# Feed-forward in groups of three for the last 33 blocks of a two-layer graph network, and one block alone at the end

## The chip, the core and the metric

The kernel runs on one core of a Trainium2 chip. The metric is device time in microseconds (us), from the first to the last instruction of one execution, as the median of several runs. Features and weights are float32.

## What is computed

There are 10000 nodes with 512 features each and 160000 edges. The edges are sorted by destination and have one of four types. The reference, cut to what matters:

```
h   = relu(layernorm(x))
# layer 0
m   = mean over edges into n of (h[src] @ rel_W[type] + rel_b[type])
x1  = layernorm(h + h @ self_W + self_b + m)          # scaled by ln1_w, ln1_b
f   = gelu(x1 @ W1 + b1) @ W2 + b2                    # 512 -> 1024 -> 512
x   = x + layernorm(x1 + f)                           # scaled by ln2_w, ln2_b
# layer 1
h   = relu(layernorm(x))
h   = relu(h @ W_self1 + mean(h[src]) @ W_neigh1 + b1)
out = x + relu(h @ W_self2 + mean(h[src]) @ W_neigh2 + b2)
```

## The kernel before

The nodes are cut into 78 blocks of 128 rows, numbered 0 to 77, and one block of 16 rows, number 78, which is taken first. The program has four stages. The first one multiplies all nodes by the four relation matrices, and writes the table `hall_d`; it also makes the lists of edges. The second stage, which the change touches, goes over the 79 blocks: it sums the messages of a block, applies the first layer norm, the feed-forward part (gelu) and the second layer norm, and writes the input of layer 1 to `h1_d`. The third and the fourth stage are the two steps of layer 1; each one gathers rows of a table that the stage ahead of it has written in full. So the third stage can gather nothing before the last row of `h1_d` has been written.

**Gathers.** For a block, `begin` (L900) calls `gather` (L840), which issues indirect DMAs on POOL (L844): 5 lists of rows that are summed with a one-hot matrix ("others"), 11 lists with one row per node ("mine"), and every fourth and every sixteenth block one further list that serves 4 or 16 blocks (`tails`; `halves_of`, L830, splits it into a high and a low part on DVE and ACT). Every list fills a tile `rows` of 128 rows by 2 KB; in the second stage there are 28 such tiles in turn (`RINGS`). TensorE (PE) sums the others into PSUM (`sums`, L881, with the matmuls in L897), and DVE adds the 11 mine (`add`, L904, with L908).

**Slots.** The order is written out by hand (the scheduler is off in this part). The loop over the blocks from L1164 on makes one slot per block b. A slot holds, in this order: the one-hot matrices for block b+1; `second` (L1097) for what came out of the feed-forward part in the slot before; `add` for block b; the statistics of its layer norm; `products` (L1143), which is one part of a queue of feed-forward work; within it, ahead of its last call, `scaled` (L1109), that is the layer norms on ACT and DVE and the writes of `xn_d` and `h1_d`; and `begin` for block b+1. In the middle of the work of the next slot block b is turned (four transposes on PE, L1018).

**Groups.** The feed-forward part works on groups of blocks (`Group`, L1005). `up` (L1024) makes 128 of the 1024 hidden features for all blocks of the group: four matmuls with n = 128 columns per block (L1030), and one gelu on ACT (L1032). `down` (L1035) takes 8 matmuls with 512 columns per block (L1041). `parts` (L1045) cuts a group into parts, and each slot takes one part off the queue. Before, groups are four blocks; a group has four parts: 4 ups, 4 ups, 2 downs, 2 downs. A group's parts go into the queue at the end of the first slot of the next group. The last group holds blocks 76 and 77. `load_res` (L942) loads the residual rows ahead of a pair of downs; its three buffers are taken in turn.

After the loop the parts that are left are worked off (from L1201 on), with no more gathers beside them. Of the groups, the parts left at that point are: the three last parts of blocks 72 to 75 and the three parts of blocks 76 and 77.

Of the kernel before, what the change touches and what calls it, by code (L numbers as in the profile page):

```python
# [21 lines left out]
def kernel(  # L22
# [39 lines left out]
    FC = F // P  # L62
# [8 lines left out]
    full = N // P  # L71
# [528 lines left out]
    with ExitStack() as s:  # L600
# [42 lines left out]
        def turned(i, rows, c):  # L643

            r = sets[i][2]
            xg, sc, hg, hT = rows
            nc.scalar.activation(hg[:r, c, :], xg[:r, c, :], AF.Relu, bias=sc[c][1],
                                 scale=sc[c][0])
            transposed(psT, hT[:, c, :, :r], hg[:r, c, :], r)
# [162 lines left out]
    def aligned(ctxa):  # L812
# [5 lines left out]
        rest = list(range(full))  # L818
        blocks = ([full] if N % P else []) + rest

        def height(b):
            return min(P, N - b * P)
# [38 lines left out]
        def hots(b, pool, lanes=None):  # L861
            n = OT + NL if b < full else OT_LAST
            hot = pool.tile([P, OT + NL, P], F32, name="hot", bufs=2)
            if lanes is None:
                for t in range(n):
                    nc.scalar.activation(hot[:, t, :], lane, AF.Abs, bias=loc[:, b, t:t + 1],  # L866
                                         scale=-1.0)
                nc.scalar.activation(hot[:, :n], hot[:, :n], AF.Relu, bias=ones[:, :1], scale=-1.0)
                return hot
            nc.vector.tensor_tensor(hot[:, :n].bitcast(F32R),  # L870
                                    lanes[:, None, :].to_broadcast([P, n, P]),
                                    loc[:, b, :n].unsqueeze(2).to_broadcast([P, n, P]),
                                    op=OP.is_equal)
            return hot
# [25 lines left out]
        def begin(b, hot, table, pool, idle=None, split=False):  # L900
            others, mine = gather(b, table, pool, split)
            return sums(b, others, hot, idle), mine

        def add(b, pa, mine):  # L904

            r = height(b)
            for t in mine:
                nc.vector.tensor_tensor(pa[:r], pa[:r], t[:r], op=OP.add)  # L908


        with ExitStack() as s:
# [16 lines left out]
            def pair(t, b, n, name, bufs):  # L928

                return (gp.tile([P, 2, D], F32, name=name, bufs=bufs)[:height(b), :n],  # L930
                        rows_of(t, (b, n, height(b))))

            def load(b):
                if b < full and b % 2:
                    return
                n = 2 if b < full else 1
                v, at = pair(xs_d, b, n, "xs", 3)
                nc.sync.dma_start(v, at)
                for c in range(n):
                    nodes[b + c] = v[:, c, :]  # L940

            def load_res(b, n):  # L942
                i = len(taken) % 3
                taken.append(b)
                v, at = pair(xr_d, b, n, "xr", 1)
                if i:
                    v = halves[i - 1][:height(b), :n]
                nc.sync.dma_start(v, at)
                for c in range(n):
                    xrs[b + c] = v[:, c, :]  # L950
                xrs[b, n] = v
# [13 lines left out]
            def fetch(n, room=None):  # L965

                for k, b in enumerate(waiting[:n]):
                    i = late.index(b)
                    t = row_tile() if room is None else room[:, k, :]
                    queue = nc.sync if room is None else nc.scalar  # L970
                    queue.dma_start(t, hT_d[i * P:(i + 1) * P, :])
                    arrived.append((b, t))
                del waiting[:n]

            def residuals(n):

                for b, t in arrived[:n]:
                    po = psO.tile([P, D], F32, name="po")
                    for k in range(KC):
                        nc.tensor.matmul(po, t[:, k * P:(k + 1) * P], wself[:, k, :],  # L980
                                         start=(k == 0), stop=(k == KC - 1))
                    nc.vector.tensor_tensor(t, po, bself, op=OP.add)
                    nc.sync.dma_start(xs_d[b * P:(b + 1) * P, :], t)
                del arrived[:n]
# [20 lines left out]
            class Group:  # L1005
# [26 lines left out]
                    nc.scalar.activation(self.hid[:, f, :n], ph[:, :n], AF.Gelu,  # L1032
                                         bias=b1s[:, f:f + 1], scale=1.0)

                def down(self, b):  # L1035
                    c, r = self.bs.index(b), self.r
                    if c % 2 == 0:
                        load_res(b, min(2, len(self.bs) - c))
                    po = psO.tile([P, D], F32, name="po")
                    for f in range(FC):  # L1040
                        nc.tensor.matmul(po[:r], self.hid[:, f, c * r:(c + 1) * r], w2s[:, f, :],  # L1041
                                         start=(f == 0), stop=(f == FC - 1))
                    return b, po

                def parts(self):  # L1045

                    ups = [lambda f=f: self.up(f) for f in range(FC)]
                    downs = [lambda b=b: self.down(b) for b in self.bs]
                    return [ups[:FC // 2], ups[FC // 2:]] + [downs[i:i + 2]
                                                             for i in range(0, len(downs), 2)]  # L1050

            COLS = 8

            class Scales:
# [31 lines left out]
                def affine(self, out, v, c, r, w, to):  # L1086
# [3 lines left out]
                    nc.vector.scalar_tensor_tensor(out, v, self.rs[:r, 0, c:c + 1], to,  # L1090
                                                   op0=OP.mult, op1=OP.add)

            rests = {}
            fed, third = [], []
            now = Scales()
# [38 lines left out]
                    nc.sync.dma_start(rows_of(xn_d, (b, n, height(b))), xrs.pop((b, n)))  # L1134

            plan = [[b] for b in blocks[:len(blocks) - len(rest)]]
            plan += [rest[:-2][i:i + 4] for i in range(0, len(rest) - 2, 4)] + [rest[-2:]]
            queue = []
            turning = None
            held = begin(blocks[0], first_hot, table, gp, split=True)  # L1140
# [2 lines left out]
            def products(work, turned):  # L1143


                nonlocal fed
                got = []
                residuals(min(2, len(arrived) - len(ready)))
                for i, call in enumerate(work):
                    if i == len(work) - 1:  # L1150
                        yield
                    if i == len(work) // 2 and turned:
                        turned()
                    got.append(call())
                if not work:
                    yield
                    if turned:
                        turned()
                residuals(len(arrived) - len(ready))
                fed = [g for g in got if g]  # L1160

            i = 0
            grp = None
            for bs in plan:  # L1164
                for b in bs:
                    r = height(b)
                    if b == bs[0]:
                        before, grp = grp, Group(bs)
                    if i + 2 < len(blocks):
                        load(blocks[i + 2])  # L1170
                    if i + 1 < len(blocks):
                        hot = hots(blocks[i + 1], gp, lanes)
                    ready = []
                    if i + 2 < len(LATE):
                        if i:
                            fetch(LATE[i + 2])
                        ready = arrived[len(arrived) - LATE[i + 2]:]
                    if i == 1:
                        nc.sync.dma_start(w2s, w2.rearrange("(k p) n -> p k n", p=P))
                    got = second()  # L1180
                    pa, mine = held
                    add(b, pa, mine)
                    v = nodes[b]
                    nc.vector.scalar_tensor_tensor(pa[:r], pa[:r], rdeg[:r, b:b + 1], v[:r],
                                                   op0=OP.mult, op1=OP.add)
                    first = (b, now.stats(pa[:r], r), pa)
                    part = products(queue.pop(0) if queue else [], turning)
                    next(part)
                    now.finish()
                    scaled(got, first)  # L1190
                    next(part, None)
                    if i + 1 < len(blocks):
                        held = begin(blocks[i + 1], hot, table, gp, split=True)

                    if b == bs[0] and before:
                        queue += before.parts()
                    turning = lambda g=grp, b=b, v=v: g.turn(b, v)
                    i += 1
            turning()
            queue += grp.parts()  # L1200
            while queue or fed or third:  # L1201
                got = second()
                part = products(queue.pop(0) if queue else [], None)
# [9 lines left out]
        for step, (h_d, ws, wn, bs) in enumerate(((h1_d, ws1, wn1, bs1), (h2_d, ws2, wn2, bs2))):  # L1213
            with ExitStack() as s:
# [47 lines left out]
                before = None  # L1262
                held = begin(blocks[0], hots(blocks[0], ip), h_d, ip)
                for i, b in enumerate(blocks):
# [6 lines left out]
                    m = ip.tile([P, D], F32, name="mb")  # L1271
# [13 lines left out]
                    before = (b, po, mT)  # L1285
# [319 lines left out]
```

## Time and profile before

Every fp32 matmul of the program stands in the trace as two records.

| | |
|---|---|
| time, median of 3 runs | 6163.95 us (6160.82 to 6165.61) |
| profiled execution | 7032.07 us, span 7030.1 us, mean granted clock 0.904 |
| gathers (L844) | 3828 in all: 1716 + 858 + 786 + 393 + 50 + 25 |
| first gather of the second stage | 1206.0 us |
| last gather of the second stage ends | 3125.0 us |
| first gather of the third stage | 3239.43 us |
| pause of the gathers between the third and fourth stage | 60.07 us |
| last gather starts | 6970.74 us |

The profiled execution is longer than the runs without the profiler. The page gives busy time by engine over the whole span; the stretches of the second stage have to be read from the timeline, since the stages have different limits. "Idle before" is time that an engine spent waiting ahead of an instruction, with what ended it; "issue" is a wait for nothing that the profile shows.

### The profile page before, as it was taken

The page shows a single profiled execution, that of the slowest core. Times are in us where ns is not written, and L with a number is a line of the kernel's source. Part 1 is how long each engine was busy: PE and PEld are TensorE (multiplying, and loading weights), DVE is VectorE, ACT ScalarE, POOL GpSimd, SP SyncE. Part 2 cuts the span into 40 slices and gives each one's busy share as a digit, 9 for nine tenths or more (in the row PEclk, how much of TensorE's full clock was granted, in tenths as well). Part 3 has the DMA queues.
Part 4 walks back from the last instruction along what each step waited for, and adds up shares of the span by engine and source line. Part 5 has one row for each costly group of instructions (what it writes and reads, how often), then busy time and mean ns, then how long its engine had stood idle before and what let it go on. Part 6 is the DMA issues. An engine that isn't in the chain of part 4 may idle for free.

```text
span 7030.1 us, 55146 instructions
## 1 busy us (share of the span) xinstructions
PE 5756.5 (82%) x15103; PEld 2675.2 (38%) x15103; DVE 3683.9 (52%) x7447; ACT 1805.0 (26%) x3594; POOL 3716.9 (53%) x3927
## 2 busy tenths in 40 slices
PE   9999999788988889885777777777757777777778
PEld 4555544343433334332333333333323333333333
DVE  8889995466766667661333333333323343434334
ACT  1046660123222223221222222222212121212122
POOL 0011110566666666643666666666556666666664
PEclk9999999899999999997888888988878888898889
DMA  4333344777777777654666666666657676776764
GB/s 156 115 129 123 131 156 149 238 222 225 225 217 217 223 218 229 210 178 157 202 205 205 203 205 204 209 202 204 185 180 218 209 221 211 217 220 212 220 213 154
DMA packets 503502, 1373.79 MB, mean 195 GB/s; under 512 B 82206, under 2 KB 82206, under 8 KB 503054
## 3 DMA queue, kind: packets, MB, share of 16 engines
q0 software_dynamic: 308768, 1008.91, 47.8%
q1 hardware_dynamic: 192734, 358.11, 14.0%
q10 hardware_dynamic: 1680, 3.15, 0.1%
q8 instruction: 122, 2.00, 0.1%
q14 instruction: 198, 1.62, 0.1%
HBM read 1156.54 MB, written 213.30 MB: 195 GB/s over the span
## 4 chain that ended last, share of the span: by engine, by line
PE 61%; issue 19%; another core or an unknown queue 9%; DVE 5%; ACT 3%; DMA 2%; POOL 2%; SPq 0%; POOLq 0%; DVEq 0%; ACTq 0%
PE pa L897 14%; PE pm L774 13%; PE ph L1030 7%; PE po L1247 7%; PE po L1041 6%; PE po L1276 4%; PE pa L879 4%; DVE pa L908 3%; PE pm L678 2%; POOL rows L844 2%; PE pT L172 2%; PE po L980 1%; DMA rows<-h_d,row 1%; PE pT L1018 0%
## 5 line engine op out<-in xcount | busy, mean ns | idle before, releaser
L908 DVE TENSOR_TENSOR pa<-pa,rows 128x512 f32<-128x512 f32 x2574 | 1799.0, 699 | 2026.4 <-remote 1008.8
L844 POOL DMA_INDIRECT rows<-h_d,row x1716 | 1621.9, 945 | 1006.0 <-issue 381.8
L1247 PE MATMUL po<-wns,mTb 128*128 128x512 f32 (+1 forms) x1264 | 737.9, 738 | 836.5 <-issue 653.0
L897 PE MATMUL pa<-rows,hot 128*128 128x512 f32 (+1 forms) x2358 | 1116.1, 613 | 101.1 <-issue 91.1
L844 POOL DMA_INDIRECT rows<-hall_d,row x858 | 822.1, 958 | 497.0 <-issue 196.8
L844 POOL DMA_INDIRECT rows<-h_d,orow x786 | 743.0, 945 | 413.3 <-issue 222.1
L1247 PEld LDWEIGHTS po<-wns,mTb 128*128 128x128 f32 (+1 forms) x1264 | 290.2, 238 | 1270.5 <-issue 1043.6
L897 PEld LDWEIGHTS pa<-rows,hot 128*128 128x128 f32 (+1 forms) x2358 | 456.1, 194 | 706.6 <-issue 680.9
L1030 PE MATMUL ph<-x1T,w1s 128*128 128x512 f32 (+2 forms) x1344 | 582.5, 585 | 74.1 <-ACT hid L1032 37.1
L1276 PE MATMUL po<-wss,hTb 128*128 128x512 f32 (+1 forms) x1264 | 596.3, 616 | 39.6 <-issue 24.5
L1041 PE MATMUL po<-w2s,hid 128*128 128x512 f32 (+1 forms) x1264 | 581.3, 609 | 47.2 <-issue 45.1
L844 POOL DMA_INDIRECT rows<-hall_d,orow x393 | 373.2, 950 | 393.5 <-PE pm L678 203.4
L173 ACT COPY mTb<-pT 128x512 f32<-128x512 f32 (+1 forms) x158 | 91.8, 581 | 1769.5 <-remote 1381.7
L879 PE MATMUL pa<-wss,ident 128*128 128x512 f32 x936 | 427.5, 593 | 0.0
L1030 PEld LDWEIGHTS ph<-x1T,w1s 128*128 128x128 f32 x1344 | 255.5, 198 | 372.5 <-issue 319.3
L1041 PEld LDWEIGHTS po<-w2s,hid 128*128 128x128 f32 (+1 forms) x1264 | 239.5, 193 | 341.9 <-issue 337.3
L513 POOL DMA_INDIRECT win<-rec_d,at x79 | 81.5, 1031 | 529.0 <-PE pe L538 348.2
L1276 PEld LDWEIGHTS po<-wss,hTb 128*128 128x128 f32 (+1 forms) x1264 | 235.9, 197 | 293.1 <-issue 271.1
L866 ACT ACTIVATE hot<-lane,loc 128x128 f32<-128x128 f32 x1098 | 337.8, 392 | 0.0
L774 PE MATMUL pm<-wrel,hT 128*128 128x512 f32 x624 | 296.5, 597 | 0.0
L774 PE MATMUL pm<-wrel,s 128*128 128x512 f32 x624 | 293.3, 592 | 0.0
L897 PE MATMUL pa<-tail,hot 128*128 128x512 f32 x624 | 293.2, 592 | 0.0
(307 smaller groups left out, 6117.9 us busy)
## 6 DMA issues: line engine op xcount, KB each, us to landing
hall_d<-p SPq DMA_DIRECT2D x156, 256.0 KB
hall_d<-u SPq DMA_DIRECT2D x156, 256.0 KB
hb<-h_d SPq DMA_DIRECT2D x156, 256.0 KB
rows<-h_d,row POOLq DMA_INDIRECT x1716
xg<-in_x_dram SPq DMA_DIRECT2D x39, 512.0 KB
xr_d<-xg SPq DMA_DIRECT2D x39, 512.0 KB
xs<-xs_d SPq DMA_DIRECT2D x39, 512.0 KB
h_d<-h SPq DMA_DIRECT2D x39, 512.0 KB
```

The costliest lines, as they stand in the source:

```text
L172: nc.tensor.transpose(p[:, k, :r], rows[:, k * P:(k + 1) * P], ident[:r, :r])
L678: nc.tensor.matmul(pm, a[:, k, :], w[:, k, :], start=(k == 0), stop=(k == KH - 1))
L774: nc.tensor.matmul(pm, a[:, k, :], w[:, k, :], start=(k == 0), stop=(k == KH - 1))
L844: nc.gpsimd.indirect_dma_start(out=t[:n], out_offset=None, in_=table, in_offset=bass.IndirectOffsetOnAxis(ap=idx, axis=0))
L866: nc.scalar.activation(hot[:, t, :], lane, AF.Abs, bias=loc[:, b, t:t + 1], scale=-1.0)
L879: nc.tensor.matmul(p, ident, w, start=True, stop=True)
L897: nc.tensor.matmul(pa[:r], h, v, start=(i == 0), stop=(i == len(work) - 1))
L908: nc.vector.tensor_tensor(pa[:r], pa[:r], t[:r], op=OP.add)
L1030: nc.tensor.matmul(ph[:, :n], w1s[:, k, f * P:(f + 1) * P], self.xT[:, k, :n], start=(k == 0), stop=(k == KC - 1))
L1041: nc.tensor.matmul(po[:r], self.hid[:, f, c * r:(c + 1) * r], w2s[:, f, :], start=(f == 0), stop=(f == FC - 1))
L1247: nc.tensor.matmul(po[:r], mT[:, k, :r], wns[:, k, :], start=False, stop=(k == KC - 1))
L1276: nc.tensor.matmul(po[:r], hT[:, k, :r], wss[:, k, :], start=(k == 0), stop=False)
```

## The change

Blocks 0 to 43 stay in groups of four. Blocks 44 to 76 become eleven groups of three, and block 77 is a group alone. A group of three has three parts: 5 ups; 3 ups and one down; 2 downs. The residual rows are loaded for one block and then for two. A group of one has 4 ups, 4 ups, and one down. In addition a slot takes a second part where, after its first, the queue still holds at least as many parts as the group that was queued last has. That is so in one slot: in the slot of block 48 the last part of blocks 40 to 43 (2 downs) is followed by the first part of blocks 44 to 46 (5 ups).

```diff
-                def down(self, b):
+                def down(self, b, n=0):
                     c, r = self.bs.index(b), self.r
-                    if c % 2 == 0:
-                        load_res(b, min(2, len(self.bs) - c))
+                    if n:
+                        load_res(b, n)
...
                     ups = [lambda f=f: self.up(f) for f in range(FC)]
-                    downs = [lambda b=b: self.down(b) for b in self.bs]
-                    return [ups[:FC // 2], ups[FC // 2:]] + [downs[i:i + 2]
-                                                             for i in range(0, len(downs), 2)]
+                    odd, m = len(self.bs) % 2, len(self.bs)
+                    downs = [lambda b=b, n=(1 if i < odd else (i - odd + 1) % 2 * 2): self.down(b, n)
+                             for i, b in enumerate(self.bs)]
+                    if m == 3:
+                        return [ups[:5], ups[5:] + downs[:1], downs[1:]]
+                    return [ups[:FC // 2], ups[FC // 2:]] + [downs[i:i + 2] for i in range(0, m, 2)]
...
+            THREES = 11
+            assert (full - 1 - 3 * THREES) % 4 == 0
...
-            plan += [rest[:-2][i:i + 4] for i in range(0, len(rest) - 2, 4)] + [rest[-2:]]
+            cut = full - 1 - THREES * 3
+            plan += [rest[i:i + 4] for i in range(0, cut, 4)]
+            plan += [rest[i:i + 3] for i in range(cut, full - 1, 3)] + [rest[-1:]]
...
-            i = 0
+            i = newest = 0
...
-                    part = products(queue.pop(0) if queue else [], turning)
+                    work = queue.pop(0) if queue else []
+                    if len(queue) >= newest > 0:
+                        work += queue.pop(0)
+                    part = products(work, turning)
...
                     if b == bs[0] and before:
+                        newest = len(before.parts())
                         queue += before.parts()
```

## The prediction

> **What bounds the kernel now.** I read the page first, then the order of time on PE in one stretch of the second stage and at that stage's end, then POOL, then ACT at the end.
>
> ```profile
> span 7030.1 us, 55146 instructions
> PE 5756.5 (82%) x15103; PEld 2675.2 (38%) x15103; DVE 3683.9 (52%) x7447; ACT 1805.0 (26%) x3594; POOL 3716.9 (53%) x3927
> ```
>
> The shares are means over four stages, so they decide nothing here. The timeline of PE shows a slot (start, duration, idle before):
>
> ```profile
> 2653.38 7.03 PE L1030 MATMUL ph<-x1T,w1s 128*128 128x512 f32 x16
> 2660.25 0.60 PE L1018 MATMUL pT<-ident,xs 128*128 128x128 f32 x4
> 2660.68 7.03 PE L1030 MATMUL ph<-x1T,w1s 128*128 128x512 f32 x16
> 2667.15 0.80 PE L897 MATMUL pa<-upper,hot 128*128 128x512 f32 x1
> ...
> 2668.48 4.46 PE L897 MATMUL pa<-rows,hot 128*128 128x512 f32 x10
> 2672.77 7.03 PE L1030 MATMUL ph<-x1T,w1s 128*128 128x512 f32 x16
> ```
>
> From 2653.38 to 2672.77 PE never stops: a slot **needs 19.39 us of PE**. The stretch 2400 to 3139 us has 32.5 slots, 22.7 us each; 102 us of it are waits of PE of many kinds ("issue" most of all), the rest mostly records at half rate. So in the profiled execution PE is nearly the bound, with stops that no other engine's work explains.
>
> POOL is the other candidate:
>
> ```profile
> 3239.43 0.94 POOL L844 DMA_INDIRECT rows<-h_d,orow  x1 [114.43 <-DMA h_d<-h]
> 3240.68 0.94 POOL L844 DMA_INDIRECT rows<-h_d,orow  x1 [0.30 <-issue]
> ```
>
> One gather starts 1.25 us after the other. A slot has 16 gathers, and 1/4 and 1/16 for the shared lists: 16.31 x 1.25 = 20.4 us. This tells of the runs without the profiler too. Free of gathers are 1206.0 us at the start, 114.43, 60.07, and 59.4 at the end (7030.1 - 6970.74), in all 1440. With 3828 x 1.25 = 4785 that is 6225 us, which is already more than the median of 6164. So there the gathers can take **at most** (6164 - 1440) / 3828 = 1.234 us each on average, waits included, 20.13 us a slot, if the rest is as in the profile. Almost none of the profile's stops can then be left, and PE's 19.39 us stands just under POOL's 20.13. I take POOL as the pacer of a slot there, by 0.74 us at most.
>
> At the stage's end there is no gather, and PE works alone:
>
> ```profile
> 3139.09 7.03 PE L1030 MATMUL ph<-x1T,w1s 128*128 128x512 f32 x16
> ...
> 3154.11 13.90 PE L1030 MATMUL ph<-x1T,w1s 128*128 128x512 f32 x32
> 3167.84 27.63 PE L1041 MATMUL po<-w2s,hid 128*128 128x512 f32 x64
> 3195.31 3.62 PE L1030 MATMUL ph<-x1T,w1s 128*128 128x256 f32 x16
> 3199.10 5.45 PE L1030 MATMUL ph<-x1T,w1s 128*128 128x256 f32 x24 [0.18 <-ACT hid L1032]
> 3207.02 5.45 PE L1030 MATMUL ph<-x1T,w1s 128*128 128x256 f32 x24 [2.47 <-ACT hid L1032]
> 3212.31 13.90 PE L1041 MATMUL po<-w2s,hid 128*128 128x512 f32 x32
> ```
>
> The last sum (block 77) ends at 3139.09, the last down at 3226.2; ACT's last relu ends at 3235.7, and only then do h_d and, at 3239.43, the gathers follow. These **96.6 us are on the path** in full.
>
> **What the Trainium skill says.** "FP8 and Floating Point Precision", TensorE Precision Notes: true fp32 takes four passes through the array. The trace agrees so far as each matmul has two records; their spacing is what I use: 32 records in 13.90 us, the last lasting 0.59, are 0.429 us apart; 24 of n=256 in 5.45 (last 0.38) are 0.2205 apart. "TensorE: Matmul & The Clock Gate", What's actually happening: an idle window of about 3.4 us drops the array to half rate. The trace agrees: after the 2.47 us above the spacing stays 0.22, but after 3.64 us of waiting at 2716.89 weight loads come 0.85 apart. "ScalarE: Activation LUTs", What ACT_TABLE_LOAD costs: about 1283 ns; the trace has 1.28:
>
> ```profile
> 3201.63 1.28 ACT L1075 ACT_TABLE_LOAD   x1
> 3202.92 0.30 ACT L1075 ACTIVATE rs<-mv,eps 128x4 f32<-128x4 f32 x1
> 3203.66 1.52 ACT L1083 ACTIVATE h<-wself,rs 128x512 f32<-128x512 f32 x2 [0.45 <-DVE rs L1078]
> 3205.20 1.28 ACT L1032 ACT_TABLE_LOAD   x1
> ```
>
> Between two gelus stand two loads, the square root and the relus: that is what PE waits for at 3207.
>
> **The end, after.** Slot 77 now holds 2 downs (32 x 0.429 = 13.7) and two turns (0.9): 14.6. Blocks 74 to 76: 64 up records of n=384, which the trace lacks; between 0.2205 and 0.429 the line gives 0.325 (ends 0.32 and 0.34): 20.8. Their 48 down records: 20.6. Block 77 alone: 64 records of n=128: the line gives 0.117; the ups with n=16, 16 in 1.85 us, are 0.11 apart, which is the lower end, and the mean weight load of 0.19 the upper: 7.5 (7 to 12). Its down: 16 x 0.429 + 0.16 = 7.0. PE's sum is 70.5.
>
> Waits: now the ups of block 77 are shorter than ACT's work. From the start of its ups: first gelu (load 1.28, gelu about 0.37 between 0.27 for n=16 and 0.47 for n=256) at 2.9, third gelu at 4.5, load and root 6.1, DVE 0.4, one relu 0.78, load 1.28, fourth gelu ready at 9.0; the sixth up waits for it, some 3.3 us. So the last down ends at 18.8 instead of 14.5: 4.3 more, 6 if the gap brings half rate. Sum 74.8 against 87.1 before. Behind it, one block instead of two saves on DVE an affine pair and its statistics (0.75 + 0.75 + 0.87) and on ACT a relu (0.76), and may bare a table load (1.28): 9.5 becomes 7.1 to 8.4, 7.8. **The end shrinks from 96.6 to 82.6: by 14, 11 to 15 with the bounds; I take 13.**
>
> **What goes into the slots.** Ahead of the last sum the feed-forward work is that of 73 blocks instead of 72: 13.7 us. It enters in one place, the slot of block 48 (5 ups: 13.0). Triples cost 64 x 0.325 / 3 = 6.93 per block for ups, against 6.87: 30 x 0.06 = 1.9. **15.6 us more for PE**, with the slots of blocks 48 to 77, 30 of them, to win it back: 0.52 each. POOL's pace leaves 0.74 at most, 22 in all; 0.45 after 1% of other losses, 13.5, and 2 us remain late. I take 2.
>
> The added wait: the sum of block 49 stands 13 us later behind the second part; queued behind it on DVE is the add of block 49, and POOL waits for its tiles. The first tile is used again 28 gathers or 35 us later, and the sum could run about 12 us after it (7 gathers and a landing); 13 late leaves 10. The first mine tile is added about 31 us after the block's first gather and needed at 34 x 1.25 = 42. So POOL doesn't stop: zero; if that cover is thinner, up to 5.
>
> Transfers: ahead of 11 groups SP issues one load, one write of xn and one of h1 more, at 0.36 to 0.5 us, with the same bytes. The load for the single block now stands behind the writes of its slot on SP's queue, but is needed a slot later: zero beside SP's own waits for ACT's relu, the longest of which in 2400 to 3139 us lasts 36.8 us. ACT has 3 groups more of 8 gelus, but fewer table loads per block: zero under 26% busy.
>
> The sum on the profiled execution: 7032 - 13 + 2 = 7021; its stops blur the 2. The median is 868 us under it, but the end has no gathers and hardly any stops, so the same difference is set against the median: **6153**.
>
> **The rivals.**
> *PE paces the slots.* For it: the timeline, where PE runs back to back in most slots. Against: the bound of 1.234 holds for POOL only from above; if a gather takes under 1.19, PE's 19.39 is the larger. Then nothing is won back: 6164 - 13 + 15.6 = 6167; half won back 6159.
> *The split tails collide with the groups (slower).* Place: DVE. Blocks 52, 56, ... bring a new tail, whose halves come on DVE behind add (8.0), statistics (1.6), root with load (1.6), apply and affine (3): about 15 us after the last sum, while PE arrives after 14.2 + 4.3 = 18.5. With fours this slot has downs and no affines of fed blocks. With threes the slots of blocks 51, 63 and 75 have 5 ups, the root behind the fourth gelu (11.6), and two affine pairs with statistics (4.7): 21, against 17.8 for PE. 3 us each, 4.5 where two tails are split: 10 us, from the point where PE has no slack: 6167 + 10 = 6177. Where POOL paces, it is hidden.
>
> **How the numbers follow.** Forecast 6153, its own range 6147 to 6158: chance 0.54. PE paces: 0.34. Collision: 0.12. About 0.2% (12 us) is what a measurement of this kernel tells from no change; faster than 6151.6 is a little over half of the first case: 0.32. Slower than 6176.3 is two thirds of the collision: 0.08. The rest, 0.60, is within. The range 6147 to 6170 leaves out the collision and little else.
>
> **What would show it.** Right: the stretch from the last sum to the last relu is 82 to 86 us; the slot of block 48 has 27 us of products without a stop of POOL behind it; the sum of block 77 is no later than before by more than 2. Wrong: PE still behind at block 77 by over 10 us; DVE's halves awaited at blocks 52, 64 and 76; up records of n=384 over 0.34 apart; a gap in block 77's ups over 5 us.

## The result, and the profile after

The changed kernel takes **6148.31 us** (median of 12 runs, 6142.38 to 6151.56) against 6163.83 for the kernel before (12 runs, 6159.29 to 6167.8). The ratio is 0.9975, with a 95% interval of 0.9967 to 0.9983: 15.5 us less, between 10.5 and 20.3. The forecast was 6153, 11 us less, which lies inside that interval.

The first profile of the kernel before and experiments 5 to 12 fell where TensorE was granted less clock (0.90 on average instead of 0.98) and where the kernel before takes 7032 to 7053 us, so those runs are compared only with the kernel before run beside them; the profile of the kernel before that is used below (experiment 1) was taken at 0.979.

The page of the changed kernel:

```profile
span 6141.4 us, 55591 instructions
PE 5641.5 (92%) x15295; PEld 2602.8 (42%) x15295; DVE 3674.4 (60%) x7449; ACT 1800.9 (29%) x3615; POOL 3722.4 (61%) x3927
```

The count of PE's records has grown by 192 (blocks 44 to 77 are twelve groups instead of nine, with 64 up records each), its busy time has not. Where the time went is seen only in the two places that the change touches. The first is the slot of block 48, on PE (start, duration, what ran, idle before):

```profile
2235.30 14.00 PE L1041 MATMUL po<-w2s,hid 128*128 128x512 f32 x32 [0.38 <-DVE rest L1109]
2249.14 2.74 PE L1030 MATMUL ph<-x1T,w1s 128*128 128x384 f32 x8
2251.72 0.60 PE L1018 MATMUL pT<-ident,xs 128*128 128x128 f32 x4
2252.15 10.49 PE L1030 MATMUL ph<-x1T,w1s 128*128 128x384 f32 x32
2262.18 0.69 PE L897 MATMUL pa<-upper,hot 128*128 128x512 f32 x1
...
2267.70 5.32 PE L1030 MATMUL ph<-x1T,w1s 128*128 128x384 f32 x16
```

Two downs and five ups stand in one row, 27 us of products, and only then comes the sum of block 49. POOL over the same stretch:

```profile
2239.96 0.95 POOL L844 DMA_INDIRECT rows<-hall_d,row  x1 [0.30 <-DVE pa L908]
2241.22 0.95 POOL L844 DMA_INDIRECT rows<-hall_d,orow  x1 [0.30 <-DMA rows<-hall_d,row]
...
2261.22 0.95 POOL L844 DMA_INDIRECT rows<-hall_d,orow  x1 [0.30 <-issue]
...
2274.35 0.95 POOL L844 DMA_INDIRECT rows<-hall_d,row  x1 [0.30 <-DVE pa L908]
```

Between the first and the third line lie 17 gathers in 21.26 us, 1.25 each. POOL doesn't stop while PE is behind.

The second place is the end of the stage, from the last sum on. PE:

```profile
2830.83 7.03 PE L1041 MATMUL po<-w2s,hid 128*128 128x512 f32 x16
2837.70 0.60 PE L1018 MATMUL pT<-ident,xs 128*128 128x128 f32 x4
2838.13 7.03 PE L1041 MATMUL po<-w2s,hid 128*128 128x512 f32 x16
2846.15 0.66 PE L1018 MATMUL pT<-ident,xs 128*128 128x128 f32 x4 [0.98 <-ACT x1T L1020]
2846.64 15.65 PE L1030 MATMUL ph<-x1T,w1s 128*128 128x384 f32 x48
2862.55 5.43 PE L1030 MATMUL ph<-x1T,w1s 128*128 128x384 f32 x16 [0.27 <-ACT hid L1032]
2867.82 20.76 PE L1041 MATMUL po<-w2s,hid 128*128 128x512 f32 x48
2888.42 1.95 PE L1030 MATMUL ph<-x1T,w1s 128*128 128x128 f32 x16
2891.27 2.94 PE L1030 MATMUL ph<-x1T,w1s 128*128 128x128 f32 x24 [0.90 <-ACT hid L1032]
2897.42 4.57 PE L1030 MATMUL ph<-x1T,w1s 128*128 128x128 f32 x24 [3.21 <-ACT hid L1032]
2901.83 7.03 PE L1041 MATMUL po<-w2s,hid 128*128 128x512 f32 x16
```

The sum of block 77 ends at 2830.99, the last down at 2908.9. The last relu on ACT, and the first gather of the third stage on POOL, after a wait of 80.25 us where the kernel before had 94.45:

```profile
2914.47 0.81 ACT L1086 ACTIVATE h<-xr,rs 128x512 f32<-128x512 f32 x1 [0.43 <-DVE rs L1081]
```

```profile
2918.07 0.94 POOL L844 DMA_INDIRECT rows<-h_d,orow  x1 [80.25 <-DMA h_d<-h]
```

The same two places in the kernel before, in experiment 1:

```profile
2933.14 1.52 ACT L1083 ACTIVATE h<-xr,rs 128x512 f32<-128x512 f32 x2 [0.43 <-DVE rs L1078]
```

```profile
2938.38 0.94 POOL L844 DMA_INDIRECT rows<-h_d,orow  x1 [94.45 <-DMA h_d<-h]
```

From the last sum to the last relu it is **84.3 us, where it was 96.5** (there the sum of block 77 ends at 2838.2).

Set side by side with experiment 1 (the kernel before at the same clock, span 6162.7 us), the 21.3 us between the two profiled executions divide like this:

| | before (experiment 1) | after | gain |
|---|---|---|---|
| end of the sum of block 44 | 2155.8 | 2149.5 | 6.3 |
| from there to the end of the sum of block 77 | 682.4 | 681.5 | 0.9 |
| to the last relu | 96.5 | 84.3 | 12.2 |
| to the first gather of the third stage | 3.7 | 2.8 | 0.9 |
| from there to the end | 3224.3 | 3223.3 | 1.0 |

The 6.3 us of the first row aren't the change's: up to there both programs are the same, and some 4.5 us of it stand already at block 4. They are this one execution's luck (it is 5 us under its kernel's median). The other rows make 15.0, which is the 15.5 of the medians. The last row, too, is code that the change doesn't touch.

### The profile page after: what moved, and what is told of

It is laid out like the page before. It is cut to its first block, busy times and chain, and to the rows that moved or that the text cites. A ratio compares the mean times of both kernels' runs of the same rounds, so it can differ in the third digit from the quotient of the medians.

```text
span 6141.4 us, 55591 instructions
## 1 busy us (share of the span) xinstructions
PE 5641.5 (92%) x15295; PEld 2602.8 (42%) x15295; DVE 3674.4 (60%) x7449; ACT 1800.9 (29%) x3615; POOL 3722.4 (61%) x3927
## 4 chain that ended last, share of the span: by engine, by line
PE 44%; DMA 38%; DVE 6%; issue 6%; POOL 5%; ACT 1%; another core or an unknown queue 0%; SPq 0%; POOLq 0%; DVEq 0%; ACTq 0%
DMA rows<-h_d,row 20%; PE pm L774 15%; DMA rows<-h_d,orow 13%; PE pa L897 8%; PE ph L1030 7%; PE po L1041 6%; POOL rows L844 5%; PE pm L678 2%; DVE pa L908 2%; DMA rows<-hall_d,row 2%; PE po L1287 1%; PE pT L172 1%; PE po L980 1%; PE po L1258 1%; DMA tail<-h_d,srow 1%
## 5 line engine op out<-in xcount | busy, mean ns | idle before, releaser
L897 PE MATMUL pa<-rows,hot 128*128 128x512 f32 (+1 forms) x2358 | 1231.4, 638 | 347.2 <-DMA rows<-h_d,orow 324.7
L897 PEld LDWEIGHTS pa<-rows,hot 128*128 128x128 f32 (+1 forms) x2358 | 405.7, 193 | 1110.1 <-DMA rows<-h_d,orow 838.2
L1287 PE MATMUL po<-wss,hTb 128*128 128x512 f32 (+1 forms) x1264 | 581.1, 603 | 0.0
L1258 PE MATMUL po<-wns,mTb 128*128 128x512 f32 (+1 forms) x1264 | 572.2, 596 | 1.3 <-ACT mTb L173 1.3
L1030 PE MATMUL ph<-x1T,w1s 128*128 128x512 f32 (+3 forms) x1536 | 563.8, 521 | 10.2 <-ACT hid L1032 10.2
L1041 PE MATMUL po<-w2s,hid 128*128 128x512 f32 (+1 forms) x1264 | 561.7, 598 | 7.8 <-DVE rest L1109 4.6
L1283 ACT ACTIVATE mb<-pa,rdeg 128x512 f32<-128x512 f32 (+1 forms) x158 | 108.5, 687 | 1133.0 <-DVE pa L908 1129.1
L1030 PEld LDWEIGHTS ph<-x1T,w1s 128*128 128x128 f32 x1536 | 283.7, 194 | 260.8 <-issue 167.0
L1258 PEld LDWEIGHTS po<-wns,mTb 128*128 128x128 f32 (+1 forms) x1264 | 240.2, 190 | 307.0 <-issue 271.3
L897 PE MATMUL pa<-tail,hot 128*128 128x512 f32 x624 | 307.3, 610 | 44.4 <-DMA tail<-h_d,srow 39.2
```

Of the source, the lines that this page charges most:

```text
L897: nc.tensor.matmul(pa[:r], h, v, start=(i == 0), stop=(i == len(work) - 1))
L1030: nc.tensor.matmul(ph[:, :n], w1s[:, k, f * P:(f + 1) * P], self.xT[:, k, :n], start=(k == 0), stop=(k == KC - 1))
L1258: nc.tensor.matmul(po[:r], mT[:, k, :r], wns[:, k, :], start=False, stop=(k == KC - 1))
L1283: nc.scalar.activation(m[:r], pa[:r], AF.Copy, scale=rdeg[:r, b:b + 1])
L1287: nc.tensor.matmul(po[:r], hT[:, k, :r], wss[:, k, :], start=(k == 0), stop=False)
```

## The experiments

The theory to be tested: the gain is the shorter end; the block's worth of products that moves ahead of the last sum is absorbed by slots in which POOL, not PE, sets the pace. The rivals are those of the prediction: PE paces the slots, or the split tails collide with the groups of three.

To follow the absorption I use one measure, the **lag** of a block: the time from the issue of its last "others" gather on POOL to the end of its sum on PE. In a slot that POOL paces it is short and steady.

**1. The kernel before, once more (e1_before_again).** No edit.

> The kernel before, profiled once more, since its first profile is 868 us longer than its runs and the profile after is not. If the long profile was a disturbance: a span near 6164 us, gathers 1.25 us apart through the whole second stage, and the end from the last sum to the last relu again 96 to 97 us. If the profile after is the odd one: again about 7030 us. The theory that the end is the gain wants block 77's sum no more than 5 us from that of the kernel after (2831 us); the rival, that groups of three make the slots faster, wants it over 10 us later in the kernel before.

Measured: 6164.72 us, in the profiled execution itself. Its granted clock:

```profile
core 0: 6162.7 us, clock 0.979
```

A profiled execution can be as short as an unprofiled one. So the 7030 us of the first profile weren't the profiler's doing, and the prediction's reading of its stops (they vanish without the profiler) had the wrong cause: they come with the low clock. What the prediction drew from it stands, though: POOL paces the slots. In this trace the gathers of the whole program, without the pauses between the stages, are 1.2606 us apart on average and 1.251 in the median. The sum of block 77 ends 7.2 us later than in the changed kernel, between the two bounds that were set, but 6.3 of that stand already at block 44, ahead of all that differs.

**2. One part per slot (e2_one_part_per_slot).** The groups of three and the single block stay; the second part goes.

```diff
-                    if len(queue) >= newest > 0:
-                        work += queue.pop(0)
```

> The change without the second part in the slot of block 48; the groups of three and the single block stay. Theory (one block's products leave the end and are won back in slots that POOL paces): one part more is left for the end, 13.7 us, so the end is about 98 us and the time 6161 to 6165 us, the gain gone. Rival (the shape of the groups makes the slots faster): most of the gain stays, 6150 us.

Measured: 6159.79 us, ratio 0.9995 (0.9986 to 1.0003). The part that no slot takes stands at the end. PE there:

```profile
2838.65 7.03 PE L1041 MATMUL po<-w2s,hid 128*128 128x512 f32 x16
2848.70 0.66 PE L1018 MATMUL pT<-ident,xs 128*128 128x128 f32 x4 [3.03 <-ACT xs L1086]
2849.20 15.60 PE L1041 MATMUL po<-w2s,hid 128*128 128x512 f32 x32
```

These two downs, 15.6 us, are what the slot of block 48 takes in the changed kernel. The end is 103.7 us long, 19.4 more than after the change and 7.2 more than before it. Yet the kernel isn't slower than before: from block 44 to block 77 it takes 676.4 us instead of 682.4. Of those 6.0 us, 4.3 are a shorter lag at block 77 (4.9 instead of 9.2), the rest is mostly POOL (1.264 us per gather between the two blocks, before 1.267). The shorter lag counts once, not per slot, and these are single executions. Why the lag settles at 5 with threes and at 8 with fours wasn't isolated.

**3 and 4. Fewer and more groups of three (e3_threes_3, e4_threes_19).** The double slot is moved: late, with few slots behind it (3 groups), or early, with many (the same edit with 19).

```diff
-            THREES = 11
+            THREES = 3
```

> Three groups of three instead of eleven: the slot with two parts is that of block 72, and 5 slots are left behind it instead of 29. The end is the same, 84 us. Theory: at 0.75 us a slot some 4 us of 13 are won back, PE is 8 to 10 us late at block 77 instead of 3, and the time is 6153 to 6157 us. If PE needs no winning back (it had slack of its own): 6148. If PE paces and nothing was ever won back with eleven groups: 6147, a little less than with eleven for want of the 24 blocks in threes.

> Nineteen groups of three: the slot with two parts is that of block 24, with 53 slots behind it. Theory: all is won back either way, 6147 to 6150 us, as with eleven. Rival (groups of three make the slots faster): 24 blocks more in threes, so some 8 us less, 6140. If groups of three cost PE 0.06 us a block on the path, or more by the split tails: 6150 to 6155.

Measured: with 3 groups 6161.38 us, ratio 0.9997 (0.9988 to 1.0005); with 19 groups 6145.85 us, ratio 0.9972 (0.9962 to 0.9982). The end is the same in both (83.1 and 84.6 us), so the end alone doesn't give the gain. With 24 more blocks in threes than the changed kernel, 19 groups are 2.5 us faster, and the two intervals overlap; the rival that threes make every slot faster wanted 8. The lag tells the rest:

| lag at block, us | 28 | 36 | 44 | 48 | 49 | 52 | 56 | 60 | 64 | 68 | 73 | 75 | 77 |
|---|---|---|---|---|---|---|---|---|---|---|---|---|---|
| before (experiment 1) | | | | 8.6 | 10.4 | 8.3 | 7.4 | 8.0 | 8.1 | 7.6 | 8.9 | 6.9 | 9.2 |
| after (11 groups) | | | | 8.7 | **21.6** | 20.2 | 16.3 | 11.8 | 9.7 | 7.5 | 4.9 | 5.1 | 7.9 |
| one part per slot | | | | 9.4 | 12.6 | 8.1 | 7.4 | 5.8 | 7.2 | 8.3 | 5.4 | 4.9 | 4.9 |
| 3 groups | | | | 8.8 | 8.7 | 7.6 | 7.9 | 7.8 | 8.9 | 7.7 | **20.6** | 18.7 | 20.8 |
| 19 groups | **20.1** | 13.0 | 6.3 | 6.9 | 5.4 | 8.1 | 5.9 | 6.9 | 8.8 | 5.8 | 5.1 | 4.8 | 7.9 |

In each kernel the double slot puts some 13 us into the lag (with 19 groups 22.4 us at block 25, after 8.9 at block 24); where slots follow, it is gone 16 to 20 slots later: in the changed kernel 21.6 at block 49, 7.5 at block 68, 0.74 us per slot. With three groups five slots remain, and nothing at all is won back in them, where 4 us were expected; the last sum ends at 2850.5 instead of 2838.2, and these 12 us eat the 13 of the end. This is the absorption itself: at this clock, what decides is the number of slots behind the double slot.

**5 and 6. PE paces the slots (e5_before_8_lists, e6_after_8_lists).** Three gathers less per slot in both kernels, so that POOL needs 16.6 us where PE needs 19.39. The messages of these three lists are left out of the sums.

```diff
-            return others, [rows(P, row[:, b, t:t + 1]) for t in range(own(b))]
+            return others, [rows(P, row[:, b, t:t + 1]) for t in range(max(own(b) - 3 * split, 0))]
```

> The kernel before with 8 instead of 11 lists of one row per node in the second stage; the messages of those three lists are left out of the sums there. POOL then needs 13.3 x 1.25 = 16.6 us a slot, less than PE's 19.4, so PE paces the slots. The time falls by 78 x (20.5 - 19.6) = 70 us, to about 6095 us; it is the base for the next run.

> The changed kernel with the same three lists left out in the second stage. Theory (the moved products are won back only because POOL paces the slots): with PE as the pacer nothing is won back, so 12 us less at the end and 14 to 16 us more in the slots: 0 to 4 us slower than the run before it. Rival (the gain comes from the groups of three as such, or the end is shorter for another reason): again 12 to 16 us faster than it.

Measured: 6699.2 us without the change and 6745.63 with it (0.9507 and 0.957 of the kernel before beside them, which took 7052.57). **Here the same change costs 46 us**, where 0 to 4 were expected. (The first of the two falls by 353 us and not by the 70 expected: it loses the stops of the low clock as well.) Busy time by engine from the end of the sum of block 44 to that of block 77 (window, length, then PE, PEld, DVE, ACT, POOL, the granted clock, DMA share, GB/s), first without the change, then with it:

```profile
2170.00:2811.00 641.00, 641.00 (x1655) 301.63 (x1654) 470.61 (x792) 217.29 (x353) 408.06 (x425) 1.00 0.73 227
```

```profile
2166.00:2866.00 700.00, 666.34 (x1844) 340.24 (x1843) 469.56 (x793) 222.94 (x377) 404.94 (x424) 0.99 0.67 210
```

Without the change PE is busy in every one of 641 us: the slots take 77.6 us per four, 19.4 each, the need of PE that the prediction counted. With it the stretch is 60 us longer. 15.6 are the added products by the prediction's estimate, and no slot wins them back. The other 44 are mostly new stops of PE ahead of ups of the groups of three, and slow records behind some of them:

```profile
2335.12 5.24 PE L1030 MATMUL ph<-x1T,w1s 128*128 128x384 f32 x8 [5.31 <-ACT hid L1032]
...
2769.06 4.54 PE L1030 MATMUL ph<-x1T,w1s 128*128 128x384 f32 x8 [3.36 <-issue]
...
2834.78 4.54 PE L1030 MATMUL ph<-x1T,w1s 128*128 128x384 f32 x8 [4.47 <-issue]
```

Eight records of n = 384 take 2.75 us elsewhere. These stops come to 31 us. "issue" says that the profile sees nothing that PE waits for, and at 2335 ACT itself stood idle for 5.6 us ahead of the gelu with no work of another engine as its releaser. Waits for the tails' halves are only 2.4 us here. So the rival "PE paces" is right in its sign, and was priced too low where the clock is low. What stops PE there stays open, and the pair wasn't run at clock 0.98, so what it costs when PE paces without such stops wasn't measured; ahead of ups the changed kernel at clock 0.98 has no such stop in its slots.

**7, 8 and 10. Variants of the end (e7_last_ups_together, e8_twelve_threes_and_a_pair, e10_last_ups_together).** In 7 and 10 the single block's eight ups stand in one part, so that no root and relu comes between its gelus; in 8 the last group is a pair again, behind twelve threes.

```diff
+                    if self.bs == rest[-1:]:
+                        return [ups, downs]
```

```diff
-            THREES = 11
+            THREES = 12
...
-            cut = full - 1 - THREES * 3
+            cut = full - 2 - THREES * 3
...
-            plan += [rest[i:i + 3] for i in range(cut, full - 1, 3)] + [rest[-1:]]
+            plan += [rest[i:i + 3] for i in range(cut, full - 2, 3)] + [rest[-2:]]
```

> The changed kernel, but block 77's 8 ups are one part, so one round of root, relu and two table loads on ACT stands between them instead of two. Theory (PE waits for ACT in block 77's ups, 4.1 us and half-rate records behind): from the start of its ups to its last down some 15.5 us instead of 20.4, so 4 to 5 us less than the changed kernel: 6143 to 6145 us. If the root for blocks 75 and 76 holds the path instead: no change, 6148.

> Twelve groups of three and a pair at the end instead of eleven and a single block: the same feed-forward work is left at the end, but the last group has two blocks. Theory: its ups have no gap over 2.5 us, but two blocks' worth of DVE and ACT stands behind the last down (9.5 us instead of 6.4): the end is 82 to 85 us, and the time 6146 to 6150, the same as with the single block. If the single block at the end is what shortens it: 6155 or more.

> The changed kernel with block 77's 8 ups in one part. Theory: from the start of its ups to its last down 15.5 us instead of 20.4, so 4 to 5 us less than the changed kernel beside it. If the root for blocks 75 and 76 holds the path instead: no change.

Measured: 7069.72 us, ratio 1.0029 (1.0014 to 1.0043), for 7; 7065.98 us, 1.0024 (1.0013 to 1.0034), for 8; 7066.74 us, 1.0029 (1.0011 to 1.0048), for 10, which repeats 7 beside the changed kernel itself (experiment 9). All three fell at the low clock, and their totals can't be told from experiment 9's. The traces can. PE at the end of experiment 10, and then ACT:

```profile
3246.36 5.62 PE L1030 MATMUL ph<-x1T,w1s 128*128 128x128 f32 x48 [0.90 <-ACT hid L1032]
3251.83 7.03 PE L1041 MATMUL po<-w2s,hid 128*128 128x512 f32 x16
```

```profile
3267.68 0.29 ACT L1080 ACTIVATE rs<-mv,eps 128x1 f32<-128x1 f32 x1 [5.47 <-DVE mv L1074]
3268.40 0.81 ACT L1088 ACTIVATE h<-xr,rs 128x512 f32<-128x512 f32 x1 [0.42 <-DVE rs L1083]
```

The 3.21 us gap and the half rate behind it are gone, and the last down ends 71.6 us after the last sum, 5.1 less than in experiment 9. But the last relu ends 10.4 us behind it instead of 6.4: the affines of the blocks ahead, which had stood in the gap, now stand on DVE between the last down and the last relu. From sum to relu it is 81.9 us against 83.1. The gap was mostly cover for work that has to be done anyway.

In 8, with a pair at the end, PE waits 1.76 us at most for a gelu there, and two blocks' relus stand at the end:

```profile
3242.07 5.45 PE L1030 MATMUL ph<-x1T,w1s 128*128 128x256 f32 x24 [1.76 <-ACT hid L1032]
```

```profile
3269.22 1.52 ACT L1086 ACTIVATE h<-xr,rs 128x512 f32<-128x512 f32 x2 [0.43 <-DVE rs L1081]
```

From the last sum to the last relu it takes 82.8 us, as with the single block (83.1 in experiment 9) and as was expected. So what shortens the end is one block's products less behind the last sum; that the last group is a single block adds nothing that these runs show.

**9. The changed kernel at the low clock (e9_after_again).** No edit.

> The changed kernel once more, as the base of the three runs beside it. Where the kernel before takes 6164 us, it takes 6146 to 6150 us. Where the kernel before takes 7050 us, theory (nothing is won back unless POOL paces): 0 to 30 us slower than the kernel before, like the two variants that ran there; rival (the variants were the reason): faster than it by 10 us or more.

Measured: 7062.56 us against 7036.35, ratio **1.0029** (1.0013 to 1.0044): some 26 us slower in the medians, 9 to 31 by the interval. Its end is shorter by 13.3 (83.1 instead of the 96.5 of the first profile), so more than that is lost ahead of it. Between the sums of blocks 44 and 77 its trace is 21.6 us longer than the first profile, but it is 19.6 us longer up to block 44 too, where both programs are the same: single executions at the low clock differ by that much. The lag tells who paces: from block 44 on it is 26 to 43 us in the first profile, where experiment 1 has 6 to 10. There PE, with its stops, is behind by about as much as POOL's 28 tiles allow (an estimate: 28 x 1.25 = 35 us). Some of what the changed kernel loses is in the trace, on PE at blocks 52, 64 and 76:

```profile
2561.30 0.80 PE L897 MATMUL pa<-upper,hot 128*128 128x512 f32 x1 [5.58 <-ACT upper L837]
...
2857.10 0.80 PE L897 MATMUL pa<-upper,hot 128*128 128x512 f32 x1 [7.67 <-ACT upper L837]
...
3157.42 0.79 PE L897 MATMUL pa<-upper,hot 128*128 128x512 f32 x1 [8.97 <-ACT upper L837]
```

In the middle of its sum PE waits for the upper half of a new tail: the collision of the prediction's second rival, in the three places that it named, 22 us together where 10 were written. The first profile has no such wait at these blocks, and in experiment 8, whose groups of three begin at other blocks, the two long ones stand at blocks 48 and 72 (13.1 and 9.3 us). The changed kernel at clock 0.98 waits there as well (blocks 52 and 64; block 76 has 0.75):

```profile
2328.35 0.50 PE L897 MATMUL pa<-upper,hot 128*128 128x512 f32 x1 [2.72 <-ACT upper L837]
...
2565.45 0.50 PE L897 MATMUL pa<-upper,hot 128*128 128x512 f32 x1 [2.49 <-ACT upper L837]
```

6 us, which the lag has taken up again a few slots later. These are no sign of the groups of three, though: at that clock the kernel before waits for an upper half at each of its tails from block 48 to 76, 11.9 us in all, and the changed kernel 6.6.

**11. The tails split at the start of a slot (e11_tails_first).** The order of the gathers stays, but the halves of a new tail are made ahead of the slot's other work, so that they don't stand behind the group of three on DVE and ACT.

```diff
-                if b < full and b % n == 0:
+                if not split and b < full and b % n == 0:
...
+        def new_tails(b, table, pool):
+
+            for lv, n in enumerate(SPANS):
+                if b < full and b % n == 0:
+                    t = row_tile()
...
+                    tails[lv] = halves_of(t, lv, pool)
...
+                    if i + 1 < len(blocks):
+                        new_tails(blocks[i + 1], table, gp)
```

> The changed kernel, but the halves of a new tail are made at the start of a slot, ahead of the add, instead of behind the affines; the gathers keep their order. Theory of the collision (sums of blocks 52, 64 and 76 wait for the halves behind two affine pairs): these three waits go; where POOL paces only the one at block 76 is late enough to count: 2 to 3 us less than the changed kernel; where PE paces up to 37 us less. Rival (those sums wait for landings): no change.

Measured: 7028.03 us, ratio 0.9982 (0.9966 to 0.9998), beside 1.0029 for the unedited changed kernel. Those two intervals don't meet; the medians are 34.5 us apart. The sum of block 52 in its trace:

```profile
2508.42 4.46 PE L905 MATMUL pa<-rows,hot 128*128 128x512 f32 x10
2512.31 0.80 PE L905 MATMUL pa<-upper,hot 128*128 128x512 f32 x1
2512.95 0.40 PE L905 MATMUL pa<-lower,hot 128*128 128x512 f32 x1
```

No wait stands ahead of "upper", here or at blocks 64 and 76. So the collision is real, and this edit removes it. That it decides the sign at the low clock isn't shown: the three waits are 22 of the 34.5 us, and the edit reaches every tail, also those of the groups of four, where the first profile has such waits too (11 us in all). In the traces of experiments 9 and 11, 19 of 39 us lie ahead of block 44. The kernel before wasn't run with this edit, so part of the gain may be had without the change. Whether it is worth anything at clock 0.98 wasn't measured.

**12. Three edits together (e12_threes_19_tails_first_last_ups).** 19 groups of three, the tails first, and the last ups together: the edits of experiments 4, 11 and 10.

> Nineteen groups of three, the halves first, and block 77's ups in one part, all in one. If the three parts add: 2 + 2.5 + 4.5 us less than the changed kernel, 6138 to 6142 where that takes 6148. If the halves first hold up the add (they wait for the landing of the tail on DVE): 6148 or more.

Measured: 7047.65 us, ratio 1.0007 (0.9989 to 1.0025). Together they do no better than the tails alone: the median is 20 us above that of experiment 11, though no sum behind block 44 waits for a half in its trace either. The interval overlaps those of experiments 9 and 11, so nothing is decided by this run.

Only experiments 2, 3 and 4 ran at clock 0.98, and none of them clearly beats the changed kernel: the intervals of 19 groups (6145.85 us) and 11 (6148.31 us) overlap.

## Why the prediction held

**What paces a slot.** The forecast rested on POOL standing over PE, and that was right. PE's need of 19.39 us per slot is right to the digit (experiment 5). POOL's 20.4 us came out as 20.7 (682.4 us for 33 slots in experiment 1). The bound between them, at most 1.234 us per gather, is **wrong**: the trace has 1.2606. It subtracted pauses of the first profile that are longer at the low clock: at the end of the second stage 114.4 us, in experiment 1 94.5; between the third and fourth stage 60 against some 16; behind the start of the last gather 59.4 against 19.4. The error made POOL's lead over PE too small: 0.74 us a slot instead of 1.3.

That the lag then fell by 0.74 us a slot all the same, from block 49 to 68 of the changed kernel, is luck. POOL took 20.68 us a slot there. Groups of three cost PE nothing: where nothing stops it, three slots take 58.2 us (blocks 54 to 57), 19.40 each, so the 1.9 us counted for them don't show. But of the lead of 1.28, stops took 0.34 (6.5 us in 19 slots, 5.2 of them waits for upper halves), and PE's busy time was 19.60 a slot instead of 19.40, in part because records ran slowly behind a stop, as at block 64:

```profile
2561.83 1.13 PE L897 MATMUL pa<-rows,hot 128*128 128x512 f32 x2 [1.24 <-DMA rows<-hall_d,orow]
2565.45 0.50 PE L897 MATMUL pa<-upper,hot 128*128 128x512 f32 x1 [2.49 <-ACT upper L837]
...
2566.49 7.00 PE L1030 MATMUL ph<-x1T,w1s 128*128 128x384 f32 x16
```

These 16 records take 5.32 us elsewhere. 20.68 - 19.60 - 0.34 leaves 0.74: a lead that was too small, and a loss to the tails that was called hidden, offset each other.

**The end.** Predicted 82.6 us, measured 84.3:

| step | predicted | measured |
|---|---|---|
| slot 77: two downs, two turns | 14.6 | 15.7, with 0.98 of waiting for ACT |
| ups of blocks 74 to 76 | 20.8 | 21.2 (0.323 us per record against 0.325; 0.27 of waiting) |
| their downs | 20.6 | 20.6 |
| ups of block 77 with ACT's waits | 11.8 | 13.4 |
| its down | 7.0 | 7.0 |
| behind the last down | 7.8 | 6.4 |

The spacings that the trace of before didn't have, by the line through n = 256 and n = 512, are 0.323 for n = 384 and 0.116 for n = 128, as estimated. The gap ahead of the sixth up is 3.21 us against "some 3.3". The half rate that was held open came: 24 records take 4.57 us behind the gap and 2.94 ahead of it. The Trainium skill ("TensorE: Matmul & The Clock Gate", What's actually happening) ties half rate to an idle window of about 3.4 us; here 3.21 us were enough, and 2.47 in the kernel before weren't, while at block 64 two stops of 1.24 and 2.49 us close together were, so no single length divides the cases. The chain behind the last down is shorter because DVE and ACT had done the other blocks' layer norms in that very gap, as experiment 10 shows from the other side.

**Into the slots.** The block's products stand where they were put, and raise the lag by 13 (8.7 to 21.6). "0.52 per slot needed, 0.74 there, 2 us left late" came out as 0.74 per slot and nothing left over the kernel before at block 77 (7.9 against 9.2): the stretch from block 44 to 77 is 0.9 us shorter, not 2 longer. POOL's gathers give 1.5 us there (1.264 us each instead of 1.267), and the lag's rise from one end to the other (6.4 to 7.9, before 8.3 to 9.2) takes 0.6 back. A difference of 3 us in single executions may be chance: up to block 44 the same code differed by 6.3. Against groups of three without the double slot (experiment 2) 5.1 us are lost, 3.0 of them a longer lag at block 77; the other 2.1 are a lag that was longer in experiment 2 already at block 44, ahead of all that differs. With the 0.9 us between the last relu and the first gather, which the sum didn't hold (one block's rows are written instead of two), and the end's 12.2 instead of 13, these terms make 14.0 of the 15.5.

**POOL doesn't stop at the double slot**: right, its gathers run on at 1.25. **Transfers and ACT at nothing**: no wait of PE for the loads of SP or for a gelu shows in the slots of the changed kernel at clock 0.98.

**The rivals.** "PE paces", 6167, is what happens where POOL is made short: no win-back. Its +2.6 us was far too low there, since it held nothing for the new stops. The collision is in the three places named, and halves awaited there were one of the prediction's own signs of being wrong; at clock 0.98 the lag took the waits up. Its price of 3 us was about right at two of the places there (2.7, 2.5, 0.75), and too low by half or more at 0.90 (5.6 to 9.0). What it had wrong is that the kernel before is free of such waits: where POOL paces, it has more of them (11.9 us between blocks 44 and 77, against 6.6).

The forecast was 4.7 us too long, less than the measurement can tell from nothing (the interval of the gain is 9.8 us wide); it put the likeliest outcome within 0.2%, while the 15.5 us are 0.25%, with an interval (0.17% to 0.33%) that reaches over that bound.

## What to carry to other kernels

Work that is moved from an end where one engine stands alone into a steady stretch can be won back there if another engine paces that stretch, and if enough of it is left: divide the work moved by the slack per slot, and count the slots behind it. Where the engine that gets the work is itself the pacer, the gain can turn round, as in experiments 6 and 9; both ran at the low clock, with stops of PE of their own, so the two causes weren't separated. To see who paces, make the pacing engine shorter in an experiment (here three gathers less), or follow the lag. Before a gap at the end is closed, look at what the other engines do in it: here 5 us less on PE gave 1.2 on the path.

## What the runs showed that was not expected

- The same program on the same kind of core took 6164 us and some 7040 us, at mean granted clocks of 0.979 and 0.90. PE's busy time differs by only 2% (5647 against 5757 us); the difference lies mostly in stops. In experiment 1, 78 distances between gathers, the pauses between stages left out, were over 1.3 us, and they added 41 us in all; in the first profile there were 372, and they added 807. POOL's instruction itself takes 0.946 us in both (median). What brings the low clock about wasn't found.
- At the low clock a PE that had always work had no stops in the stretch compared: in experiment 5 it was busy 641.00 of 641.00 us and was granted 1.00 there. The stops came in the kernels whose PE also had real waits; that these bring the stops about isn't shown.
- Where a stop of a few us stood ahead of fp32 records, slow records followed after 3.21 us at clock 0.98 (24 in 4.57 instead of 2.94 us); at the low clock eight records of n = 384 took 4.54 instead of 2.75 us after 3.36 and 4.47 us, but in the same run 24 of them took 8.01 us after a stop of 3.17, and 7.91 elsewhere.
